# Values of a cross-attention layer made eight heads at a time, with 512 moving columns

## The chip, the cores and the metric

The kernel runs on one core of one Trainium2 chip. The metric is the device time of one execution in microseconds (us); the times of several runs are given with their median.

## What is computed

A cross-attention block and a feed-forward block with low-rank experts, both with a residual, over 16 sequences of 64 tokens and width 512 (1024 tokens in all). Cut to what matters here:

```python
def _L0_xattn_ref(hidden_q, hidden_kv, attention_mask, position_bias, Wq, Wk, Wv, Wo):
    B, S, D, H, DH = (2, 128, 512, 32, 128)
    q = (hidden_q @ Wq).reshape(b, lq, h, dh)
    k = (hidden_kv @ Wk).reshape(b, lk, h, dh)
    v = (hidden_kv @ Wv).reshape(b, lk, h, dh)
    score = jnp.einsum('bqhd,bkhd->bhqk', q, k) * scale + position_bias
    ...
    ctx = jnp.einsum('bhqk,bkhd->bqhd', probs, v).reshape(b, lq, h * dh)
    return ctx @ Wo
x = x + _L0_xattn_ref(_layernorm(x, axis=-1), ctx_4096, ...)
x = x + _L0_ffn_ref(_layernorm(x, axis=-1), ...)
```

`Wk` and `Wv` are 512 x 4096 (32 heads of 128), so keys and values are each a product of 1024 x 512 by 512 x 4096. The change concerns the values.

## The kernel before

**Arithmetic.** Every large product is made with float32r operands that are split into a high and a low part (`split`, L67: ACT copies the high part, DVE subtracts to get the low one), and three matmuls, high x high, low x high and high x low (`mm3`, L219). On top of that, the products of weights and tokens are made by a Winograd-Strassen scheme (`winograd`, L176): each matrix is cut into 2 x 2 blocks, seven block products are made instead of eight (`ORDER`: 1, 2, 6, 5, 7, 4, 3), and sums of blocks are taken before (classes `Tokens`, L115, and `Weights`, L149) and after (`post`, L180). A pass works on n output blocks side by side. Block k has an x bank in PSUM for products 1, 6, 7 and 4, a z bank for product 2 and a y bank for products 5 and 3. After product 1, ACT copies x to `u`; after 2, DVE adds u and z to the block c11; after 6, ACT copies x to `u2`; after 7, ACT copies x to `u3` and DVE adds u3 and y to c22; after 4, ACT copies x out as c21; after 3, DVE adds u2 and y to c12. The next product into a bank waits for the copy before it.

**Stages.** `cT` holds the context, transposed. Its token parts `t1` to `t7` (high and low) are made once. Then the heads are taken by quads, eight of them.

- Keys of a quad (`mm_weights`, L225, two blocks): the weights stand in the array, 512 tokens move; 7 x 2 x 2 x 3 = 84 matmuls of 512 columns. Blocks are stored to the DRAM tiles `kd` (L303).
- Values of a quad (`mm_tokens`, L232, two blocks, each of two column ranges `r`): 128 tokens stand in the array, 256 weight columns move; 7 x 2 x 2 x 2 x 3 = 168 matmuls of 256 columns. Blocks are stored to the DRAM tiles `vd` (L309), one of which holds two heads.

Quad 0's keys and values are made product by product in turn (L321), while the token parts are still being made. For quads 1 to 7 (L332) keys come first, then values; values of quad 7 come after this loop, interleaved with the first queries (L494). During the values of quads 2 to 5, the eight tiles of x are loaded and normalized (`x_tile`, L284) and transposed on PE (`x_turn`, L294): one after product 6 and one after product 7. `xT` is read later, on POOL, to make the token parts of x for the queries.

After that come attention and output projection in a loop over 16 pairs of heads (L504), where keys, values, queries' weights and biases are loaded again, and then the feed-forward block (from L544).

**What sets the order.** The order on PE in this part is that of the program text (`manual_schedule` for PE). On ACT, DVE, POOL and SP a scheduler sets a fixed order when the kernel is built. All loads and stores here are issued on SP. Buffers come from pools: `raw` (10) for loaded weights, `sum` (4) for sums of weight blocks, `g` (18) for split weights, `o` (9) for token differences at this stage, `sn` (8) for u copies, `ob` (8) for finished blocks, `v` (5) for tiles of x and later values. PSUM has eight banks: six of the pool `psp` (`bank`) and two of the pool `pss` (`small_bank`, used by x's transposes and by z and y of quad 0's values).

Of the kernel before, what the change touches and what calls it, by code (L numbers as in the profile page):

```python
# [9 lines left out]
F32 = mybir.dt.float32  # L10
F32R = mybir.dt.float32r
# [7 lines left out]
P = 128  # L19
# [23 lines left out]


@with_exitstack
def xattn_ffn_kernel(ctx: ExitStack, tc: tile.TileContext, x, ctxT, wq, wk, wv, wo, fside, mask,
                     base_wT, base_b, arT, router_b, lora_b, expert_map, out):
    nc = tc.nc
    scale = 1.0 / math.sqrt(128.0)
# [8 lines left out]
        pools[n] = ctx.enter_context(tc.tile_pool(name=n, bufs=BLOCKS[n]))  # L58
    psp = ctx.enter_context(tc.tile_pool(name="psp", bufs=6, space=PSUM))

    def bank():
        return psp.tile([P, 512], F32, tag="ps", name="ps")

    def blk(tag, name, dt=F32, shape=(P, 512)):
        return pools[tag].tile(list(shape), dt, tag=tag, name=name)

    def split(hi, lo, src, lo_eng=None):  # L67
        nc.scalar.copy(hi, src)  # L68
        (lo_eng or nc.vector).tensor_tensor(lo, src, hi.bitcast(F32), ALU.subtract)  # L69
# [30 lines left out]
            nc.tensor.transpose(ps[:, kc * P:(kc + 1) * P], xn[:, kc * P:(kc + 1) * P], ident)  # L100

    kd = [dram.tile([P, TOK], F32, tag=f"kd{h}", name=f"kd{h}") for h in range(H)]
    vd = [dram.tile([P, NT, 256], F32, tag=f"vd{h}", name=f"vd{h}") for h in range(H // 2)]

    with ExitStack() as actx:
        pss = actx.enter_context(tc.tile_pool(name="pss", bufs=2, space=PSUM))
# [5 lines left out]
        def small_bank(name):  # L112
            return pss.tile([P, 512], F32, tag="s", name=name)

        class Tokens(dict):  # L115


            def __init__(self, src, eng):
                self.eng, self.t = eng, {}
                lo, hi = slice(0, HALF), slice(HALF, TOK)  # L120
                self.b = {(i, j): [src[:, 2 * i + k, c] for k in range(2)] for i in range(2)
                          for j, c in enumerate((lo, hi))}
# [26 lines left out]
        class Weights(dict):  # L149
# [5 lines left out]
            def summed(self, a, b, op, name):  # L155
                r = blk("sum", name, F32, (P, 2, self.cols))
                self.eng.tensor_tensor(r, a, b, op)  # L157
                return r
# [12 lines left out]
            def all(self, order=ORDER):  # L171
                for i in order:
                    self.make(i)
                return self

        def winograd(mm, n, emit, yzbank=bank, order=ORDER):  # L176

            xb, zb, yb, u, u2, u3 = ({} for _ in range(6))

            def post(i, k):  # L180
                if i == 1:
                    u[k] = blk("sn", "u")
                    nc.scalar.copy(u[k], xb[k])
                elif i == 2:
                    c = blk("ob", "c11")
                    nc.vector.tensor_tensor(c, u[k], zb[k], ALU.add)
                    emit(0, 0, k, c)
                elif i == 6:
                    u2[k] = blk("sn", "u2")
                    nc.scalar.copy(u2[k], xb[k])  # L190
                elif i == 7:
                    u3[k] = blk("sn", "u3")
                    nc.scalar.copy(u3[k], xb[k])
                    c = blk("ob", "c22")
                    nc.vector.tensor_tensor(c, u3[k], yb[k], ALU.add)
                    emit(1, 1, k, c)
                elif i == 4:
                    c = blk("ob", "c21")
                    nc.scalar.copy(c, xb[k])
                    emit(1, 0, k, c)  # L200
                elif i == 3:
                    c = blk("ob", "c12")
                    nc.vector.tensor_tensor(c, u2[k], yb[k], ALU.add)
                    emit(0, 1, k, c)

            for i in order:
                for k in range(n):
                    if i == 1:
                        xb[k] = bank()
                    elif i == 2:  # L210
                        zb[k] = yzbank()
                    elif i == 5:
                        yb[k] = yzbank()
                    b = xb if i in (1, 6, 7, 4) else zb if i == 2 else yb
                    mm(i, k, b[k], i in (1, 2, 5))
                    post(i, k)
                yield i
# [7 lines left out]
        def mm_weights(t, g):  # L225
            def mm(i, k, o, first):
                for kc in range(2):
                    mm3(o, [a[:, kc, k * P:(k + 1) * P] for a in g[i]], [b[:, kc] for b in t[i]],
                        first and kc == 0, kc == 1)
            return mm  # L230

        def mm_tokens(t, g):  # L232
            def mm(i, k, o, first):
                for r in range(2):
                    c = slice((2 * k + r) * P, (2 * k + r + 1) * P)
                    for kc in range(2):
                        mm3(o[:, r * 256:(r + 1) * 256], [a[:, kc, c] for a in t[i]],
                            [b[:, kc] for b in g[i]], first and kc == 0 and r == 0, kc == 1)
            return mm

        def load_raw(src):
            r = {}
            for i, j in ((0, 0), (0, 1), (1, 0), (1, 1)):
                r[i, j] = blk("raw", "raw", F32, (P, 2, 256))
                nc.sync.dma_start(out=r[i, j], in_=src[i, j])
            return r

        def gran4(r, eng):
            return Weights(r[0, 0], r[0, 1], r[1, 0], r[1, 1], 256, eng)
# [34 lines left out]
        def x_tile(t):  # L284
            nonlocal xT
            if xT is None:
                xT = ax.tile([P, KC, TOK], F32, tag="ax", name="xT")
            xt = blk("v", "xt")
            nc.sync.dma_start(out=xt, in_=x[t])
            xn = blk("v", "xn")  # L290
            norm(sm, [xn], [xt])
            return xn

        def x_turn(t, xn):  # L294
            ps = small_bank("pst")
            transposed(ps, xn)
            b, g = divmod(t, 4)
            dst = xT.rearrange("p k (g a b s) -> p g b k a s", g=4, a=2, b=2)[:, g, b]
            nc.scalar.copy(dst, ps.rearrange("p (k a s) -> p k a s", k=KC, a=2))

        def emit_k(q):
            def emit(i, j, k, c):
                nc.sync.dma_start(out=kd[4 * q + 2 * i + k][:, j * HALF:(j + 1) * HALF], in_=c)  # L303
            return emit

        def emit_v(q):
            def emit(i, j, k, c):
                t = 4 * j + 2 * k
                nc.sync.dma_start(out=vd[2 * q + i][:, t:t + 2, :], in_=c.rearrange("p (t d) -> p t d", t=2))  # L309
            return emit  # L310

        tc_ = Tokens(cT, nc.vector)
# [1 line left out]
        with tc.manual_schedule(engines={nc.tensor.engine}):  # L314
# [2 lines left out]
                tc_.make(i)  # L317
                gv.make(i)
            keys = winograd(mm_weights(tc_, gk), 2, emit_k(0))
            values = winograd(mm_tokens(tc_, gv), 2, emit_v(0), lambda: small_bank("yzv"))  # L320
            for n in range(7):  # L321
                if n < 6:
                    gk.make(ORDER[n + 1])
                    tc_.make(ORDER[n + 1])
                    gv.make(ORDER[n + 1])
                else:
                    rk = load_raw(wk[1])
                    rv = load_raw(wv[1])
                    gk = gran4(rk, nc.vector).all()
                next(keys)  # L330
                next(values)
            for q in range(1, NQ):  # L332
                gv = gran4(rv, nc.vector).all()
                if q + 1 < NQ:
                    rk = load_raw(wk[q + 1])
                    rv = load_raw(wv[q + 1])
                for i in winograd(mm_weights(tc_, gk), 2, emit_k(q)):
                    pass
                if q + 1 < NQ:
                    gk = gran4(rk, nc.vector).all()  # L340
                if q == 2:
                    nc.vector.tensor_scalar(maskb, m8, -1.0, BIG, ALU.add, ALU.mult)  # L342
                    nc.vector.tensor_reduce(valid, m8, AX.X, ALU.max)
                    nc.vector.tensor_copy(emf, emi)
                    for e in range(E):
                        nc.vector.tensor_scalar(oneh[:, e, :], emf, float(e), 2.0, ALU.is_equal, ALU.mult)
                if q + 1 < NQ:
                    for i in winograd(mm_tokens(tc_, gv), 2, emit_v(q)):
                        if 2 <= q < 6:
                            t = 2 * (q - 2)  # L350
                            if i in (1, 5):
                                xn = x_tile(t + (i == 5))
                            elif i in (6, 7):
                                x_turn(t + (i == 7), xn)


            acc = None
# [17 lines left out]
            def load_v(p):  # L375
                v = []
                for w in range(4):
                    v.append(blk("v", "v", F32, (P, 2, 256)))
                    nc.sync.dma_start(out=v[w], in_=vd[p][:, 2 * w:2 * w + 2, :])
                return v  # L380

            def load_o(p):
# [326 lines left out]
```

## Time and profile before

| | |
|---|---|
| runs (3) | 793.59, 793.68, 794.07 us; median 793.68 |
| profiled execution, its own time | 795.94 us |
| its span | 794.2 us |
| PE busy in the span | 778.5 us |
| DVE, ACT, POOL busy | 589.1, 413.0, 144.0 us |
| keys of quad 2 on PE | 89.08 to 108.14 us |
| values of quad 1 on PE | 68.92 to 89.08 us |
| first attention scores on the chain that ended last | 338.07 us |

The profile is of one execution. Matmuls overlap, so their durations add up to more than the time they take; the distance from one start to the next is what a matmul costs in a dense stretch. A row of the timeline reads: start, duration, engine, line, operation, output<-inputs, shape, count, and in brackets the idle time before it with what ended that.

### The profile page before, as it was taken

What the parts mean: (1) busy time and instruction counts of PE and PEld (TensorE: products, weight loads), DVE (VectorE), ACT (ScalarE), POOL (GpSimd) and SP (SyncE); (2) the same over time, 40 slices, a digit from 0 to 9 for tenths busy, and PEclk for the clock granted to TensorE, in tenths of its full rate; (3) what the DMA queues carried; (4) which work ended last, traced back from release to release, by engine and by line L of the source; (5) the groups of instructions that cost most, each with busy time, mean ns of one, the idle gap of its engine ahead of it and who ended that gap; (6) DMA issues with size and microseconds to landing.
All of it is one profiled execution on the core that took longest, in us unless ns stands there. A gap on an engine that the chain in (4) does not pass through costs nothing.

```text
span 794.2 us, 18002 instructions
## 1 busy us (share of the span) xinstructions
PE 778.5 (98%) x6944; PEld 673.7 (85%) x6944; DVE 589.1 (74%) x1056; ACT 413.0 (52%) x1154; POOL 144.0 (18%) x146
## 2 busy tenths in 40 slices
PE   7999999999999999999999999999999999999997
PEld 6988999999999999978888888888888888888786
DVE  6997656555557555678878787878777887878986
ACT  6655444454444444674664566455655466456342
POOL 1011000000006002033311332033202230210352
PEclk9999999999999999999999999999999999999999
DMA  7675545454545543375553364335553455241011
GB/s 269 207 244 200 173 159 186 160 186 160 185 160 171 174 159 133 127 237 170 173 170 90 129 186 161 107 124 171 161 157 97 147 175 171 84 148 56 1 42 66
DMA packets 66374, 120.56 MB, mean 152 GB/s; under 512 B 7536, under 2 KB 8176, under 8 KB 66288
## 3 DMA queue, kind: packets, MB, share of 16 engines
q1 hardware_dynamic: 66288, 119.42, 45.8%
q8 instruction: 54, 0.88, 0.5%
q14 instruction: 32, 0.26, 0.1%
HBM read 83.74 MB, written 35.65 MB: 150 GB/s over the span
## 4 chain that ended last, share of the span: by engine, by line
PE 88%; DVE 7%; ACT 2%; DMA 2%; issue 1%; POOL 0%; SPq 0%; ACTq 0%; DVEq 0%; POOLq 0%
PE ps L222 77%; PE pss L404 4%; PE ps L436 4%; PE pst L423 2%; PE yzv L222 1%; ACT p L412 1%; DMA cT<-in_ctxT 1%; DVE o L637 1%; DVE pr L606 1%; DVE x2l L69 1%; DVE nb L94 1%; DVE gl L69 0%; PE pst L100 0%; DVE we L608 0%; DMA so<-in_wo 0%
## 5 line engine op out<-in xcount | busy, mean ns | idle before, releaser
L68 ACT CAST gh<-s 128x512 fp32r<-128x512 f32 (+1 forms) x128 | 65.6, 514 | 147.3 <-PE ps L222 139.3
L69 DVE TENSOR_TENSOR gl<-s,gh 128x512 fp32r<-128x512 f32 (+1 forms) x128 | 73.3, 572 | 44.5 <-ACT gh L68 44.4
L452 DVE TENSOR_TENSOR acc<-acc,ps 128x512 f32<-128x512 f32 x128 | 86.1, 681 | 21.6 <-PE ps L222 20.7
L412 ACT ACTIVATE p<-p,nm 128x64 f32<-128x64 f32 x256 | 85.5, 336 | 31.6 <-DVE nm L409 31.6
L222 PE MATMUL ps<-wh,oh 128*128 128x512 f32 x256 | 101.4, 397 | 0.0
L222 PE MATMUL ps<-wl,oh 128*128 128x512 f32 x256 | 99.9, 391 | 0.0
L222 PE MATMUL ps<-wh,ol 128*128 128x512 f32 x256 | 99.7, 390 | 0.0
L157 POOL TENSOR_TENSOR s<-rq 128x256 f32<-128x256 f32 x32 | 25.2, 788 | 290.4 <-DMA rq<-in_wq 206.5
L395 POOL TENSOR_TENSOR bm<-bm,maskb 128x512 f32<-128x512 f32 x32 | 50.0, 1582 | 73.1 <-DVE maskb L342 40.8
L69 DVE TENSOR_TENSOR gl<-raw,gh 128x512 fp32r<-128x512 f32 x48 | 34.1, 712 | 31.4 <-ACT gh L68 31.4
L222 PEld LDWEIGHTS ps<-wl,oh 128*128 128x128 f32 x256 | 48.1, 188 | 10.1
L222 PEld LDWEIGHTS ps<-wh,ol 128*128 128x128 f32 x256 | 48.1, 188 | 9.9 <-DVE ol L69 0.5
L222 PEld LDWEIGHTS ps<-wh,oh 128*128 128x128 f32 x256 | 48.1, 188 | 9.5
L68 ACT CAST gh<-raw 128x512 fp32r<-128x512 f32 x48 | 29.7, 621 | 47.8 <-PE ps L222 36.6
L69 DVE TENSOR_TENSOR ol<-ps,oh 128x512 fp32r<-128x512 f32 x64 | 39.8, 683 | 15.6 <-ACT oh L68 15.6
L412 ACT ACTIVATION_READ_ACCUMULATOR p<-p,nm 128x1 f32 x256 | 48.1, 188 | 0.0
L69 DVE TENSOR_TENSOR gl<-rq,gh 128x256 fp32r<-128x256 f32 x48 | 32.9, 687 | 11.4 <-ACT gh L68 11.4
L479 DVE TENSOR_TENSOR q<-u,ps 128x512 f32<-128x512 f32 x48 | 32.6, 680 | 10.6 <-PE ps L222 10.6
L68 ACT CAST oh<-ps 128x512 fp32r<-128x512 f32 x64 | 33.1, 590 | 7.7 <-PE ps L436 7.7
L92 POOL TENSOR_TENSOR rs<-rs,nhalf 128x1 f32<-128x1 f32 x16 | 9.5, 595 | 152.1 <-DVE rs L91 109.2
L404 PEld LDWEIGHTS pss<-kT,q 128*64 128x64 f32 x1024 | 31.2, 138 | 5.6 <-PE ps L222 5.0
L436 PEld LDWEIGHTS ps<-pt,v 64*64 64x64 f32 x2048 | 31.4, 135 | 3.3 <-ACT gh L68 2.2
(226 smaller groups left out, 2273.7 us busy)
## 6 DMA issues: line engine op xcount, KB each, us to landing
kd<-c SPq DMA_DIRECT2D x64, 256.0 KB, 2.6
vd<-c SPq DMA_DIRECT2D x64, 256.0 KB, 2.8
v<-vd SPq DMA_DIRECT2D x64, 256.0 KB, 4.3
kT<-kd SPq DMA_DIRECT2D x64, 256.0 KB, 5.4
raw<-in_wk SPq DMA_DIRECT2D x32, 256.0 KB, 3.0
raw<-in_wv SPq DMA_DIRECT2D x32, 256.0 KB, 3.0
bm<-in_fside SPq DMA_DIRECT2D x32, 256.0 KB, 5.7
rq<-in_wq SPq DMA_DIRECT2D x32, 256.0 KB, 5.5
```

The lines of the kernel that those rows point to most:

```text
L68: nc.scalar.copy(hi, src)
L69: (lo_eng or nc.vector).tensor_tensor(lo, src, hi.bitcast(F32), ALU.subtract)
L92: nc.gpsimd.tensor_tensor(rs, rs, nhalf[:, 0:n], ALU.pow)
L157: self.eng.tensor_tensor(r, a, b, op)
L222: nc.tensor.matmul(o, lhsT=a, rhs=b, start=first and n == 0, stop=last and n == 2, skip_group_check=True)
L395: nc.gpsimd.tensor_tensor(bm, bm, maskb, ALU.add)
L404: nc.tensor.matmul(ps[a * S:(a + 1) * S, t, :], lhsT=qT[n // 8][:, c], rhs=kT[n // 8][:, c], start=True, stop=True)
L412: nc.scalar.activation(p[:, t, :], p[:, t, :], AF.Exp, bias=nm[:, t:t + 1], accum_out=sme[:, t:t + 1])
L423: nc.tensor.transpose(ps[:, g * P:(g + 1) * P], p[:, 2 * g:2 * g + 2, :].rearrange("p t k -> p (t k)"), ident)
L436: nc.tensor.matmul(ps[b][d:d + S, u * S:(u + 1) * S], lhsT=v[u // 2][r, u % 2, c], rhs=pt[r, u, :], start=True, stop=True)
L452: nc.vector.tensor_tensor(acc[:, t, :], acc[:, t, :], ps, ALU.add)
L479: nc.vector.tensor_tensor(self.blocks[key], s[u], b[bk], ALU.add)
```

## The change

The values of quads 1 to 6 are made for two quads together, in three passes. A new class `OctWeights` loads the weights of eight heads (`wvo`, eight loads of 256 KB per pass) into buffers of the pool `o`, sums their blocks and splits them; each of its matrices is two tiles of 128 x 512, one for each half of the depth. The new `mm_oct` has 128 tokens standing and 512 weight columns moving. A pass has four blocks; z and y of blocks 0 and 1 lie in `psp`, those of blocks 2 and 3 in `pss`. The fourth sum of weight blocks is written over the second. Keys of two quads come first, then the values of both. `vd` becomes one tile per quad, and a block is stored to it in rows of 1 KB. Values of quad 0 and of quad 7 stay as they are. Loading, normalization and transposes of x move to the keys of quads 3 to 6: tiles are asked for after products 1 and 6 and transposed after products 5 and 3.

```diff
-    vd = [dram.tile([P, NT, 256], F32, tag=f"vd{h}", name=f"vd{h}") for h in range(H // 2)]
+    vd = [dram.tile([P, 2, NT, 256], F32, tag=f"vd{q}", name=f"vd{q}") for q in range(NQ)]
...
+        class OctWeights(dict):
+            def __init__(self, src):
+                self.a = {}
+                for i, j in ((0, 0), (0, 1), (1, 0), (1, 1)):
+                    self.a[i, j] = [blk("o", "raw8") for _ in range(2)]
+                    for kc in range(2):
+                        nc.sync.dma_start(out=self.a[i, j][kc], in_=src[i, j, :, kc])
+            def summed(self, a, b, op, r=None):
+                r = r or [blk("sum", "s8") for _ in range(2)]
+                for kc in range(2):
+                    nc.vector.tensor_tensor(r[kc], a[kc], b[kc], op)
+                return r
+            def make(self, i):
+                a = self.a
+                if i == 6:
+                    self.s1 = self.summed(a[1, 0], a[1, 1], ALU.add)
+                    self.s2 = self.summed(self.s1, a[0, 0], ALU.subtract)
+                src = (a[0, 0] if i == 1 else a[0, 1] if i == 2 else self.s2 if i == 6 else self.s1 if i == 5 else
+                       self.summed(a[0, 0], a[1, 0], ALU.subtract) if i == 7 else a[1, 1] if i == 4 else
+                       self.summed(a[0, 1], self.s2, ALU.subtract, self.s2))
+                self[i] = [[blk("g", f"g{c}", F32R) for _ in range(2)] for c in "hl"]
+                for kc in range(2):
+                    split(self[i][0][kc], self[i][1][kc], src[kc])
...
+        def mm_oct(t, g):
+            def mm(i, k, o, first):
+                for kc in range(2):
+                    mm3(o, [a[:, kc, k * P:(k + 1) * P] for a in t[i]], [b[kc] for b in g[i]],
+                        first and kc == 0, kc == 1)
+            return mm
...
-                nc.sync.dma_start(out=vd[2 * q + i][:, t:t + 2, :], in_=c.rearrange("p (t d) -> p t d", t=2))
+                nc.sync.dma_start(out=vd[q][:, i, t:t + 2, :], in_=c.rearrange("p (t d) -> p t d", t=2))
+            return emit
+        def emit_oct(q):
+            def emit(i, j, k, c):
+                nc.sync.dma_start(out=vd[q + i][:, :, 4 * j + k, :], in_=c.rearrange("p (w d) -> p w d", w=2))
             return emit
...
-            for q in range(1, NQ):
-                gv = gran4(rv, nc.vector).all()
-                if q + 1 < NQ:
-                    rk = load_raw(wk[q + 1])
-                    rv = load_raw(wv[q + 1])
-                for i in winograd(mm_weights(tc_, gk), 2, emit_k(q)):
-                    pass
-                if q + 1 < NQ:
-                    gk = gran4(rk, nc.vector).all()
+            def keys_of(q, g):
+                xn = {}
+                for i in winograd(mm_weights(tc_, g), 2, emit_k(q)):
+                    if 3 <= q < 7:
+                        t = 2 * (q - 3)
+                        if i in (1, 6):
+                            xn[i] = x_tile(t + (i == 6))
+                        elif i == 5:
+                            x_turn(t, xn[1])
+                        elif i == 3:
+                            x_turn(t + 1, xn[6])
+            for q in range(1, NQ - 1, 2):
+                rk = load_raw(wk[q + 1])
+                go = OctWeights(wvo[q // 2])
+                gn = gran4(rk, nc.vector).all()
+                keys_of(q, gk)
+                rk = load_raw(wk[q + 2])
+                go.all()
...
+                keys_of(q + 1, gn)
+                gk = gran4(rk, nc.vector).all()
+                for i in winograd(mm_oct(tc_, go), 4, emit_oct(q), lambda k: bank() if k < 2 else small_bank("yzv")):
+                    pass
+            gv = gran4(load_raw(wv[1]), nc.vector).all()
+            keys_of(NQ - 1, gk)
...
-                if q + 1 < NQ:
-                    for i in winograd(mm_tokens(tc_, gv), 2, emit_v(q)):
-                        if 2 <= q < 6:
-                            t = 2 * (q - 2)
-                            if i in (1, 5):
-                                xn = x_tile(t + (i == 5))
-                            elif i in (6, 7):
-                                x_turn(t + (i == 7), xn)
```

More of the change, by code (lines that the diff above doesn't have):

```diff
@@ L45, in xattn_ffn_kernel @@
 @with_exitstack
-def xattn_ffn_kernel(ctx: ExitStack, tc: tile.TileContext, x, ctxT, wq, wk, wv, wo, fside, mask,
+def xattn_ffn_kernel(ctx: ExitStack, tc: tile.TileContext, x, ctxT, wq, wk, wv, wvo, wo, fside, mask,
                      base_wT, base_b, arT, router_b, lora_b, expert_map, out):
@@ L59, in xattn_ffn_kernel, with bank @@
     psp = ctx.enter_context(tc.tile_pool(name="psp", bufs=6, space=PSUM))
-    def bank():
+    def bank(k=None):
         return psp.tile([P, 512], F32, tag="ps", name="ps")
@@ L174, in all @@
                 return self
+        class OctWeights(dict):
[21 more added lines that the diff above has]
+                    split(self[i][0][kc], self[i][1][kc], src[kc])
+            def all(self):
+                for i in ORDER:
+                    self.make(i)
+                return self
         def winograd(mm, n, emit, yzbank=bank, order=ORDER):
@@ L210, in winograd @@
                     elif i == 2:
-                        zb[k] = yzbank()
+                        zb[k] = yzbank(k)
                     elif i == 5:
-                        yb[k] = yzbank()
+                        yb[k] = yzbank(k)
                     b = xb if i in (1, 6, 7, 4) else zb if i == 2 else yb
@@ L319, in xattn_ffn_kernel @@
             keys = winograd(mm_weights(tc_, gk), 2, emit_k(0))
-            values = winograd(mm_tokens(tc_, gv), 2, emit_v(0), lambda: small_bank("yzv"))
+            values = winograd(mm_tokens(tc_, gv), 2, emit_v(0), lambda k: small_bank("yzv"))
             for n in range(7):
@@ L327, in xattn_ffn_kernel @@
                     rk = load_raw(wk[1])
-                    rv = load_raw(wv[1])
                     gk = gran4(rk, nc.vector).all()
@@ L331, in xattn_ffn_kernel @@
                 next(values)
-            for q in range(1, NQ):
-                gv = gran4(rv, nc.vector).all()
-                if q + 1 < NQ:
-                    rk = load_raw(wk[q + 1])
-                    rv = load_raw(wv[q + 1])
-                for i in winograd(mm_weights(tc_, gk), 2, emit_k(q)):
-                    pass
-                if q + 1 < NQ:
-                    gk = gran4(rk, nc.vector).all()
-                if q == 2:
+            def keys_of(q, g):
[16 more added lines that the diff above has]
+                go.all()
+                if q == 1:
                     nc.vector.tensor_scalar(maskb, m8, -1.0, BIG, ALU.add, ALU.mult)
@@ L378, in load_v @@
                     v.append(blk("v", "v", F32, (P, 2, 256)))
-                    nc.sync.dma_start(out=v[w], in_=vd[p][:, 2 * w:2 * w + 2, :])
+                    nc.sync.dma_start(out=v[w], in_=vd[p // 2][:, p % 2, 2 * w:2 * w + 2, :])
                 return v
@@ L684 @@
         "wk": c(arr(L0_xattn_Wk).reshape(2, 2, P, NQ, 2, 256).transpose(3, 4, 0, 2, 1, 5)),
-        "wv": c(arr(L0_xattn_Wv).reshape(2, 2, P, NQ, 2, 256).transpose(3, 4, 0, 2, 1, 5)),
+        "wv": c(arr(L0_xattn_Wv).reshape(2, 2, P, NQ, 2, 256)[:, :, :, (0, NQ - 1)].transpose(3, 4, 0, 2, 1, 5)),
+        "wvo": c(arr(L0_xattn_Wv)[:, 512:-512].reshape(2, 2, P, NQ // 2 - 1, 2, 512).transpose(3, 4, 0, 2, 1, 5)),
         "wo": c(arr(L0_xattn_Wo).reshape(H // 2, 2, P, D)),
```

## The prediction

> **What bounds the kernel now.** I read the first and fourth part of the page, then a table by stage, then the matmuls one by one where the heads' values are made. The page: TensorE (PE) is busy nearly all the time, and the chain that ended last runs through it.
>
> ```profile
> span 794.2 us, 18002 instructions
> PE 778.5 (98%) x6944; PEld 673.7 (85%) x6944; DVE 589.1 (74%) x1056; ACT 413.0 (52%) x1154; POOL 144.0 (18%) x146
> ...
> PE 88%; DVE 7%; ACT 2%; DMA 2%; issue 1%; POOL 0%; SPq 0%; ACTq 0%; DVEq 0%; POOLq 0%
> ```
>
> The table of busy time by stretch (window: length, then PE, weight load, DVE, ACT, POOL, clock, DMA share, GB/s) shows where PE is not busy, and how much room the others have while values are made (108.14 to 128.30 is one such pass):
>
> ```profile
> 0.00:20.00 20.00, 14.59 (x70) 12.33 (x71) 13.62 (x22) 12.36 (x21) 2.25 (x8) 1.00 0.78 267
> ...
> 60.00:64.00 4.00, 2.88 (x13) 2.08 (x12) 2.50 (x12) 2.01 (x4) 0.55 (x1) 1.00 0.45 137
> 108.14:128.30 20.16, 20.16 (x170) 20.15 (x169) 11.83 (x21) 11.00 (x19) 0.88 (x1) 1.00 0.48 162
> ```
>
> Between 64 and 325 us PE has no gap: there a microsecond less of PE work is a microsecond less of span, as long as nothing else becomes late. What a matmul costs is not its duration (they overlap) but the distance from start to start. The timeline of PE where keys (512 moving columns) give way to values (256):
>
> ```profile
> 107.46 0.39 PE L222 MATMUL ps<-t3h,gh 128*128 128x512 f32 x1
> 107.69 0.39 PE L222 MATMUL ps<-t3h,gl 128*128 128x512 f32 x1
> 107.92 0.39 PE L222 MATMUL ps<-t3l,gh 128*128 128x512 f32 x1
> 108.14 0.28 PE L222 MATMUL ps<-gh,t1h 128*128 128x256 f32 x1
> 108.26 0.28 PE L222 MATMUL ps<-gh,t1l 128*128 128x256 f32 x1
> 108.38 0.28 PE L222 MATMUL ps<-gl,t1h 128*128 128x256 f32 x1
> ```
>
> Over whole passes: values of quad 1 run from 68.92 to 89.08, 20.16 us for 168 matmuls, 0.1200 each; keys of quad 2 from 89.08 to 108.14, 19.06 us for 84, 0.2269 each. Twice 0.1200 is 0.2400: two 256-column matmuls cost 0.0131 us more than one of 512. Each matmul carries some 0.013 us whatever its width.
>
> [...]
>
> **The change part by part.**
>
> *Matmuls.* Six quads' values go: 6 x 168 = 1008 matmuls of 256 columns, 6 x 20.16 = 120.96 us. Three passes for eight heads come, each 7 products x 4 token blocks x 2 halves of the depth x 3 = 168 of 512 columns: 3 x 168 x 0.2269 = 114.36 us. Stationary and moving operands are the same float32r tiles as in the keys' and values' passes, so 0.2269 is taken (bounds: 0.2267, the spacing in steady flow, to 0.2290, that of the 512-column matmuls at 63.7 us when the operands had just been made: 114.26 to 115.42). **Sum: -6.60 us** (-6.70 to -5.54). The compiled order of the changed program confirms it: PE has 504 rows fewer.
>
> *Evictions, splits and sums* (ACT copies of 0.58 and 0.62 us, DVE of 0.68 to 0.71): as many and as wide as before, 953 rows on DVE in both orders, POOL's unchanged. They lie beside PE: in the pass above DVE is busy 11.83 and ACT 11.00 of 20.16 us; per quad this now falls into 19.06 (62% and 58%). Cost 0. If the cover were gone, each late one would stop PE by its lateness.
>
> *PSUM.* The eight-head pass has four x blocks and four z or y blocks open, which is all eight banks: none is spare. I went through the changed program's order with its waits, and counted the matmuls between the last one that an eviction (with all that stands before it on its engine) depends on, and the one that needs it. In the eight-head passes that is 18 or more (18 x 0.2269 = 4.1 us for one or two operations of 0.6 to 0.7). The least anywhere is 6 (1.36 us): the u3 copy between products 7 and 4 of the keys, as before. Cost 0, to 1.1 per border in a rival below.
>
> *The split ring.* g has 18 buffers; a product of the eight-head pass takes 4 instead of 2, so splits run 4.5 products ahead (24.5 us) instead of 9 (25.9). Cost 0.
>
> *Weight loads* of values: 48 DMAs of 256 KB on SP before and after; wvo's rows are 2 KB like wv's. They go to the nine o buffers, which hold the token differences until quad 0 is split. The eighth load of the first pass stands on SP behind the store of kd3's c21 block (about 41 us before), and lands in about 3.0 us (row of in_wv), 7.4 at the worst that any DMA of vd took: 44 to 49. Its first reader stands in DVE's order where the sum at 55.24 stood. Cost 0; the price of lateness is a rival. The last quad's wv load now comes after the third pass, 19 us of keys ahead of its use. The eight token differences on POOL (244.9 to 257 before) now queue for o buffers behind the third pass's weights; they are first read at 311.0, so some 20 us of delay is free.
>
> *Value stores*: 48 of 256 KB, now in 1 KB rather than 2 KB runs. [...] upper bound, twice: 5.6. Four are issued per product of 5.45 us and there are eight ob buffers, so even 5.6 holds nobody. Cost 0.
>
> *Transposes of x.* Four transposes for each of 8 tiles, as before, now within keys, directly before product 7. Their cost on PE:
>
> ```profile
> 116.66 0.28 PE L222 MATMUL ps<-gl,t6h 128*128 128x256 f32 x1
> 116.78 0.60 PE L100 MATMUL pst<-ident,xn 128*128 128x128 f32 x4
> 117.13 0.36 PE L222 MATMUL ps<-gh,t5h 128*128 128x256 f32 x1
> ```
>
> 0.35 us and a slow first matmul, in both places: difference 0. On ACT, though, the copy to xT (0.59) and, for two of the tiles, a next tile's normalization (0.82) now stand before u3. Counting from the start T of the transposes: the transposes end at T+0.60, so xT may start at T+0.65 (the 0.05 is the usual step from PE's end to ACT), the normalization at T+1.13, u3 at T+1.96 (also when product 7's first block is ready), done T+2.5; PE wants it at T+0.43+12x0.227 = T+3.15. Spare 0.6 us. Its statistics come from a DMA issued a tile earlier, 8 to 11 us before. Cost 0, to about 1 us for each of four tiles.
>
> *Left as it is*: the start, the attention stage, the tail, and the one stall in this stage:
>
> ```profile
> 61.80 0.16 DVE L94 SCALAR_TENSOR_TENSOR nb<-mv,rs 128x1 f32<-128x1 f32 x1 [0.73 <-POOL rs L92]
> 61.99 0.81 ACT L96 ACTIVATE xn<-xt,nb,rs 128x512 f32<-128x512 f32 x1 [2.08 <-DVE nb L94]
> 62.71 0.56 ACT L193 COPY u<-ps 128x512 f32<-128x512 f32 x1
> ...
> 63.33 0.50 PE L222 MATMUL ps<-t4h,gh 128*128 128x512 f32 x1 [1.12 <-ACT u L193]
> ```
>
> The u3 copy waits behind x tile 0's normalization, that behind DVE, which had worked without a gap since about 20 us. The changed order has the same sequence there, with s8 sums in place of s sums: the 1.12 us stay.
>
> **Sum.** Profiled execution 795.94 us (span 794.2 and 1.7 around it): 795.94 - 6.60 = 789.34, span 787.6. It lies 2.26 above the median of the runs, 793.68; on the median: **787.1**. A measurement of this kernel can tell about 0.2%, 1.6 us, from no change.
>
> **The rivals.**
>
> *Better: the stall goes too.* If the other load order relieves DVE before 62 us, 1.12 us more: 786.0. Against: same order of work on DVE. 7%.
>
> *Bank borders.* PE waits at the entry and exit of each eight-head pass, six times up to 1.12 (the one late eviction that the trace has): 793.8 in full, 790.4 at half. For: no bank is free. Against: the count of 18 matmuls. 12%, of which 4% within 0.2%.
>
> *Transposes hold u3.* Up to 1 us for four tiles: 788.1 to 791.1, say 789. For: 0.6 us to spare. Against: only two of the four carry a normalization. 6%.
>
> *Slower: the first pass's weights block DVE.* [...] If the eighth load lands after 55.2, DVE stands with key splits and c blocks behind it, and PE stops 1:1. It decides from 55.2 + 6.6 = 61.8 (even) and shows as slower from 63.4, 22 us after its issue; at 66 us it gives 787.1 + 10.8 = 797.9. For: 2 MB are now wanted early, beside the keys' weights, with DMA engines at 0.86 share at 40 to 44 us. Against: 6 to 11 us of margin. 7%.
>
> That the change doesn't do what it says is excluded by the 504 rows.
>
> **Numbers.** Forecast 68%, own range 786.4 to 788.2 (the matmul bounds). Range for 8 in 10: 785.8 to 790.5, leaving out the upper half of the borders' case and the slower one. Faster .68+.07+.08+.06 = 0.89; same 0.04; slower 0.07.
>
> **What would show it.** PE rows of 128x512 with t stationary spaced 0.227 us, 38.1 us a pass; no PE wait over 0.3 us between 64 and 318 us; attention's first scores about 6.6 us earlier than 338.07. Wrong, if PE waits on ACT u3 after transposes, on c blocks at a pass's border, or DVE on raw8 near 55 us; or if spacing with t stationary isn't that of the keys.

## The result, and the profile after

| | before | after |
|---|---|---|
| runs (6 each) | 792.71 to 794.07, median 793.59 us | 786.57 to 790.51, median 788.46 us |
| ratio of the times, 95% interval | | 0.9938 [0.9921, 0.9955] |
| profiled execution, its own time (span) | 795.94 (794.2) us | 787.93 (786.1) us |

The change makes the kernel 5.1 us faster by the medians, where 6.6 were forecast. Two more comparisons of the same kernels gave 0.9932 [0.9914, 0.995] and 0.9928 [0.9912, 0.9943]. The forecast amounts to a ratio of 787.1/793.68 = 0.9917: just outside the first interval, inside the other two.

Span, busy times of the engines and shares of the chain that ended last, from the page of after:

```profile
span 786.1 us, 16982 instructions
PE 770.8 (98%) x6440; PEld 646.0 (82%) x6440; DVE 586.2 (75%) x1056; ACT 414.0 (53%) x1154; POOL 143.2 (18%) x146
...
PE 86%; DVE 7%; ACT 3%; DMA 1%; issue 1%; POOL 0%; SPq 0%; DVEq 0%; ACTq 0%; POOLq 0%
```

PE has 504 instructions fewer and is 7.7 us less busy. DVE has the same number of instructions, ACT and POOL too. Now the table by stretch of after, with the columns of the forecast's table; the last three rows are the three eight-head passes:

```profile
60.00:64.00 4.00, 3.38 (x15) 2.48 (x14) 3.26 (x6) 2.80 (x5) 0.00 (x0) 1.00 0.36 131
85.87:123.95 38.08, 38.08 (x170) 31.54 (x168) 21.64 (x34) 17.26 (x30) 0.00 (x0) 1.00 0.57 177
163.83:202.01 38.18, 38.18 (x171) 31.63 (x170) 21.44 (x33) 18.17 (x32) 0.00 (x0) 1.00 0.53 175
241.90:280.08 38.18, 38.18 (x171) 31.63 (x170) 25.66 (x33) 17.47 (x31) 11.89 (x8) 1.00 0.46 150
```

The first two numbers of each pass are equal: PE is busy from end to end. Together they last 114.44 us (114.36 forecast). DVE, the busiest of the others, is busy 57 to 67% of a pass. The matmuls one by one, where keys give way to the first eight-head pass (timeline of after, PE):

```profile
85.42 0.39 PE L255 MATMUL ps<-t3h,gl 128*128 128x512 f32 x1
85.64 0.39 PE L255 MATMUL ps<-t3l,gh 128*128 128x512 f32 x1
85.87 0.39 PE L255 MATMUL ps<-gh,t1h 128*128 128x512 f32 x1
86.09 0.39 PE L255 MATMUL ps<-gh,t1l 128*128 128x512 f32 x1
```

The start-to-start distance stays 0.22 to 0.23 us across the border, whichever operand stands in the array. The waits of PE in after between 9 and 320 us (what waited, on what: us in all, times, longest):

```profile
PE ps L255 <- ACT u L226: 0.6, 1, 0.6
PE ps L255 <- DVE gl L69: 0.2, 1, 0.2
```

Neither lies at a border of a pass; between 64 and 320 us there is none. The first is the stall that the forecast left in place. It is shorter in this execution, 0.62 us where the profile before had 1.12, but its rows (timeline of after) read as before: PE waits for the u3 copy, which stands on ACT behind an x tile's normalization:

```profile
59.92 0.82 ACT L96 ACTIVATE xn<-xt,nb,rs 128x512 f32<-128x512 f32 x1 [1.57 <-DVE nb L94]
60.64 0.56 ACT L226 COPY u<-ps 128x512 f32<-128x512 f32 x1
...
61.26 0.50 PE L255 MATMUL ps<-t4h,gh 128*128 128x512 f32 x1 [0.62 <-ACT u L226]
```

**Where the time came from.** Two marks cut the profiled execution in three: the first matmul of quad 1's keys, and the first scores of attention. Both are starts on PE's timeline.

| kernel | keys of quad 1 begin | first scores | span | between the marks | after the scores |
|---|---|---|---|---|---|
| before | 48.42 | 338.00 | 794.2 | 289.58 | 456.2 |
| after | 46.84 | 329.52 | 786.1 | 282.68 | 456.6 |
| after, two other executions | 48.87, 46.31 | 331.99, 328.72 | 788.6, 784.0 | 283.12, 282.41 | 456.6, 455.2 |

Between the marks 6.90 us went. The stall lies between them, and it took 1.12 us in the profile before and 0.62 in this one: without it the difference is 6.40 us. The passes alone give 6.65. In the first experiment that undoes the width the same three passes last 121.09 us (the forecast's count was 6 x 20.16 = 120.96), and 121.09 - 114.44 = 6.65. The 0.25 us between 6.65 and 6.40 is about what the moved transposes cost (see that experiment).

The rest of the 8.1 us between these two spans can't be put down to the change. The start differs by 1.6 us between them, but the changed kernel's own starts differ by 2.6, and in the experiment that moves only the transposes, where the start is the old one, quad 1's keys begin at 46.81.

### The profile page after: what moved, and what is told of

Read it like the earlier page. It is cut to its first block, busy times and chain, and to the rows that moved or that the text cites. A ratio compares the mean times of both kernels' runs of the same rounds, so it can differ in the third digit from the quotient of the medians.

```text
span 786.1 us, 16982 instructions
## 1 busy us (share of the span) xinstructions
PE 770.8 (98%) x6440; PEld 646.0 (82%) x6440; DVE 586.2 (75%) x1056; ACT 414.0 (53%) x1154; POOL 143.2 (18%) x146
## 4 chain that ended last, share of the span: by engine, by line
PE 86%; DVE 7%; ACT 3%; DMA 1%; issue 1%; POOL 0%; SPq 0%; DVEq 0%; ACTq 0%; POOLq 0%
PE ps L255 71%; PE ps L488 4%; PE yzv L255 4%; PE pss L456 4%; PE pst L475 2%; ACT p L464 1%; DVE gl L69 1%; DMA raw<-in_wv 1%; DVE nb L94 1%; DVE o L689 1%; DVE x2l L69 0%; DVE s L157 0%; PE pst L100 0%; DMA raw<-in_wvo 0%; PE ps L636 0%
## 5 line engine op out<-in xcount | busy, mean ns | idle before, releaser
L469 DVE TENSOR_TENSOR p<-p,rc 128x512 f32<-128x512 f32 x32 | 34.5, 1078 | 1.1
L69 DVE TENSOR_TENSOR gl<-rq,gh 128x256 fp32r<-128x256 f32 x48 | 26.4, 551 | 11.4 <-ACT gh L68 11.4
```

What stands on the lines that cost most here:

```text
L469: nc.vector.tensor_tensor(p, p, rc.unsqueeze(2).to_broadcast([P, NT, S]), ALU.mult)
```

## The experiments

The theory after the result: the whole gain is the width of the matmuls in three passes; everything else in the change costs nothing, and what differs besides is the spread from execution to execution. The rivals: part of the gain comes from the order of loads and stores, or from the place of x's transposes; part of the forecast 6.6 us is given back somewhere.

### The changed kernel again

Edit: none. Six executions, then a single one, then six on another chip.

> The changed kernel once more, for a tighter interval and a second trace. Theory A (what was forecast: 504 fewer matmuls, each saving its fixed 0.013 us, all of it on the path): 6.6 us below the kernel before, 787.0 to 787.5, ratio 0.9917. Theory B (part of it is given back by waits that differ from one execution to the next, so that the median gain stays near the 5.1 us of the first six runs): 788 to 789, and the trace shows, beside passes of 38.1 us, waits of PE in the first 64 us or after 300 us that the first trace of it does not have.

> The changed kernel, one more execution for its trace. Theory A: span near 785.5, stage boundaries as in the first trace. Theory B: a different span with the difference in one place, the first 64 us (DVE without a gap there, waiting for weights or slowed while POOL works) or the entry of attention.

> The changed kernel beside the run with all values in eight-head passes, on one chip. Theory A: 787 to 789, ratio 0.992 to 0.994; the spread between executions again comes from the first 64 us and the entry of attention.

Measured: 788.8 us against 794.46 (0.9932 [0.9914, 0.995]); 785.73 for the single one; 788.86 against 794.33 (0.9928 [0.9912, 0.9943]). The first number is the one that theory B named, not theory A's 787.0 to 787.5. All 19 executions of the changed kernel lie between 785.73 and 790.51, those of the kernel before, over all comparisons, between 791.95 and 797.7: single executions of one kernel differ by 4.8 and 5.8 us, about as much as the gain. Two of the profiles show where. First the longer one's rows on PE (the first re-run, 788.6 us of span), at the start and at the old stall:

```profile
7.38 0.80 PE L255 MATMUL ps<-t1h,gh 128*128 128x512 f32 x1 [1.04 <-ACT t1h L68]
...
63.79 0.50 PE L255 MATMUL ps<-t4h,gh 128*128 128x512 f32 x1 [1.13 <-ACT u L226]
```

Then the same two matmuls in the shorter one (784.0 us of span):

```profile
6.26 0.80 PE L255 MATMUL ps<-t1h,gh 128*128 128x512 f32 x1
...
60.47 0.51 PE L255 MATMUL ps<-t4h,gh 128*128 128x512 f32 x1 [0.37 <-ACT u L226]
```

In one PE waits 1.04 us for the split of a part of the context, for which ACT had itself waited 2.07 us until it landed (0.93 in the other, where PE doesn't wait); the stall at 60 to 64 us is 1.13 us in one and 0.37 in the other. A third place comes after the first scores: 10 to 13 us behind them PE waits for a u copy and then, in most profiles, for a sum on DVE, 1.80 us together in the longer execution and 0.56 in the shorter. (The single execution's 784.0 us of span, against 786.1 in the first profile, comes mostly from here: 455.2 and 456.6 us after the first scores.) These are waits of the kind that theory B asked for. But the kernel before has them too (0.66, 1.12 and 1.41 us in its profile), so they don't show that the change gives something back.

The start comes in two kinds. In ten profiles, of both kernels and of the experiments, it has quad 0's values in it. In four of them (the kernel before, the first re-run and two experiments) two operations on DVE last 1.8 us beside POOL near 45 us, and quad 1's keys begin at 47.7 to 48.9 us; in the six others two last 1.2 us, and the keys begin at 46.3 to 47.7. The stall at 60 to 64 us was 1.1 us wherever it followed the first kind, 0.2 to 0.7 after the second. DVE has hardly a gap there, so 2 x 0.6 us more on it may well be the reason; no run sets it on purpose. The last section shows the rows.

PE's work in the start and after the first scores is the same in both kernels. (Of the loads beside it, the change takes those of quad 1's value weights out of the start, and reads the values from the new tiles.) After the first scores the executions of both take between 455.2 and 456.6 us. So a difference of two single spans (8.1 us above) says less than the stretch between the marks, which is 282.2 to 283.1 us in four executions, and 282.0 to 282.1 in all four once the stall is taken off.

### The width undone

```diff
-                for kc in range(2):
-                    mm3(o, [a[:, kc, k * P:(k + 1) * P] for a in t[i]], [b[kc] for b in g[i]],
-                        first and kc == 0, kc == 1)
+                for r in range(2):
+                    w = slice(r * 256, (r + 1) * 256)
+                    for kc in range(2):
+                        mm3(o[:, w], [a[:, kc, k * P:(k + 1) * P] for a in t[i]], [b[kc][:, w] for b in g[i]],
+                            first and kc == 0 and r == 0, kc == 1)
```

Eight heads, loads, stores, sums and transposes stay as changed; each matmul of 512 columns becomes two of 256.

> The changed kernel, but with each 512-column matmul of the eight-head passes split into two of 256: passes, buffers, banks, loads, stores and transposes stay as changed, only the 504 matmuls come back. Theory A: 6.6 us slower than the changed kernel, so level with the kernel before (ratio 0.998 to 1.002), 20.16 us more precisely 40.3 us a pass. Theory C (the gain comes from the new order of the work and of the loads in the first 64 us, not from the matmuls): nearly as fast as the changed kernel, ratio 0.994.

Measured: 794.36 us against 794.46, ratio 1.0001 [0.9993, 1.0009]. The first pass in the table by stretch of this kernel:

```profile
85.83:126.14 40.31, 40.31 (x337) 40.31 (x336) 21.43 (x33) 16.66 (x30) 0.00 (x0) 1.00 0.51 168
```

It lasts 40.31 us for 336 matmuls, 0.1200 each, as in the kernel before; the stretch between the marks is 289.37 (289.58 before). The gain is gone, all of it. That settles the main question: the width is the gain, and the other parts of the change together cost or bring less than 0.1% (the interval). The third number differs too: weight loading is busy the whole of this pass (40.31 us), and 31.5 of 38.1 us of the wide one. Half the loads go with half the matmuls, so this run doesn't tell whether the time saved is the matmuls' own or that of their weight loads.

### The transposes alone

The kernel before, with load, normalization and transposes of x moved from the values to the keys.

```diff
                 for i in winograd(mm_weights(tc_, gk), 2, emit_k(q)):
-                    pass
+                    if 3 <= q < 7:
+                        t = 2 * (q - 3)
+                        if i in (1, 6):
+                            xn[i] = x_tile(t + (i == 6))
+                        elif i == 5:
+                            x_turn(t, xn[1])
+                        elif i == 3:
+                            x_turn(t + 1, xn[6])
...
                     for i in winograd(mm_tokens(tc_, gv), 2, emit_v(q)):
-                        if 2 <= q < 6:
...
+                        pass
```

> The kernel before with one part of the change alone: loading, normalization and transposes of x moved from the values to the keys, in the places that the change gives them. Theory A: no difference, ratio 0.999 to 1.001, no wait of PE on ACT u copies after the transposes. Rival (the copy to xT and the next normalization hold the u3 copy): up to 1 us for each of four tiles, 794.5 to 797.5, with idle PE before product 4 of the keys of quads 3 to 6.

Measured: 793.95 us, ratio 1.0 [0.999, 1.0009]; no wait of PE between 64 and 320 us. In the times the move is worth nothing either way, and the feared wait doesn't come. The stretch between the marks shows a small price: 289.41 us with a stall of 0.68 in it, so 288.73 without, against 289.58 - 1.12 = 288.46 before. Nearly all of the 0.27 us lies in four passes of values behind keys with transposes, which take 20.22 to 20.23 us where the first takes 20.16; why, no run shows. Why nothing becomes late is seen in after, where the transposes begin at 134.83 (timeline of after, rows of PE, then of ACT):

```profile
134.60 0.39 PE L255 MATMUL ps<-t5l,gh 128*128 128x512 f32 x1
134.83 0.60 PE L100 MATMUL pst<-ident,xn 128*128 128x128 f32 x4
135.19 0.48 PE L255 MATMUL ps<-t7h,gh 128*128 128x512 f32 x1
...
138.04 0.39 PE L255 MATMUL ps<-t4h,gh 128*128 128x512 f32 x1
...
135.47 0.59 ACT L339 COPY xT<-pst 128x512 f32<-128x512 f32 x1
135.95 0.81 ACT L96 ACTIVATE xn<-xt,nb,rs 128x512 f32<-128x512 f32 x1
136.86 0.59 ACT L226 COPY u<-ps 128x512 f32<-128x512 f32 x1
```

From T = 134.83: xT at T+0.64, the next tile's normalization at T+1.12, u3 from T+2.03 to T+2.62, and PE needs it at T+3.21. The forecast had 0.65, 1.13, 1.96 to 2.5, and 3.15: 0.6 us to spare, in both.

### Other widths

The forecast said that each matmul carries some 0.013 us whatever its width. That is an estimate from its two distances: between 0.1200 us for 256 columns and 0.2269 for 512 lies 0.1069/256, some 1/2400 us a column, and over that 0.013 us are left at both. Two kernels test the sentence, with one execution each. The first cuts each matmul of 512 columns into four of 128 (the loop of the width's edit, with `r` in `range(4)` and `P` columns), the second into 384 and 128:

```diff
...
+                for n, w in enumerate((slice(0, 384), slice(384, 512))):
+                    for kc in range(2):
+                        mm3(o[:, w], [a[:, kc, k * P:(k + 1) * P] for a in t[i]], [b[kc][:, w] for b in g[i]],
+                            first and kc == 0 and n == 0, kc == 1)
```

> The changed kernel with each 512-column matmul of the eight-head passes split into four of 128 columns (2016 matmuls in place of 504). It tells what the 0.013 us are. Theory A (each matmul carries about 0.0133 us beside 1/2400 us per column, so 128 columns take 0.0667): a pass of 44.8 us instead of 38.1, 20 us slower in all, near 806. Rival (256 columns already stand at a floor that the load of the 128 stationary columns sets, 0.120 us whatever the width): a pass of 80.6 us, 127 us slower, near 915.

> The changed kernel with each 512-column matmul of the eight-head passes split into one of 384 and one of 128 columns: a third width. The run with four times 128 gave 0.1117 us per 128-column matmul, so the simple form (0.0133 us and 1/2400 us per column at every width) is already wrong at 128. Theory A in its narrower form [...]: 0.1733 for 384 columns and a pass of 168 x (0.1733 + 0.1117) = 47.9 us. Rival (the load always adds part of its time, the more the narrower the matmul): spacing for 384 columns above 0.178.

Measured: 899.74 and 819.06 us. The first lies at neither of the two numbers named, 806 and 915, though much nearer the second. The first pass of the kernel with four quarters, from its table by stretch:

```profile
87.25:162.30 75.05, 75.05 (x674) 75.05 (x673) 21.61 (x33) 16.65 (x30) 0.00 (x0) 1.00 0.30 97
```

672 matmuls in 75.05 us are 0.1117 us each; by the sentence they should have taken 128/2400 + 0.013 = 0.067 us. A matmul of 128 columns costs nearly what one of 256 costs (0.1200). Weight loading is busy all of the pass here, its starts 0.11 us apart like the matmuls', so its pace may be what sets that floor. But it is busy all of the pass of 256 columns too (40.31 us), and the record of one load lasts 0.19 us at 128, 256 and 512 columns alike: what holds the narrow matmuls back was not shown. The kernel with 384 and 128 has this first pass and these rows of 384 columns (table by stretch; the timeline of PE follows):

```profile
85.77:134.25 48.48, 48.48 (x338) 48.48 (x336) 21.43 (x33) 16.63 (x30) 0.00 (x0) 1.00 0.44 144
```

```profile
100.34 0.34 PE L255 MATMUL ps<-gh,t6l 128*128 128x384 f32 x1
100.52 0.34 PE L255 MATMUL ps<-gl,t6h 128*128 128x384 f32 x1
100.70 0.22 PE L255 MATMUL ps<-gh,t6h 128*128 128x128 f32 x1
```

Within a run of six, matmuls of 384 columns are 0.18 us apart, where 384/2400 + 0.0133 would be 0.1733; where the width changes, one distance is 0.23 and one 0.06. The pass of 48.48 us is over the 47.9 of the narrower theory, and its rival (more than 0.178) is met only just. The four distances in a row of equal widths are 0.112, 0.120, 0.18 and 0.227 us for 128, 256, 384 and 512 columns. No constant beside N/2400 gives them all: over it lie 0.058, 0.013, 0.020 and 0.014. What law does is left open. For this change only 256 and 512 count, and both were measured in the kernel before.

### The stall at 61 us

In the changed kernel the normalization of x's first tile waits for DVE, which has hardly a gap from 20 to 62 us. Here `nhalf`, a constant that the normalizations need, is made from a block of quad 1's keys, so that they come later; the numbers computed are the same.

```diff
-        nc.gpsimd.memset(nhalf, -0.5)
...
+                if (i, j, k) == (0, 1, 1):
+                    nc.gpsimd.tensor_scalar(nhalf, c[:, 0:NT], 0.0, -0.5, ALU.mult, ALU.add)
```

> The changed kernel, with the exponent of the normalizations of x made from a block of quad 1's keys, so that no normalization can stand ahead of those keys' u3 copies on ACT (numbers that are computed stay the same). Theory A (the wait at 61 us comes from that normalization alone): the 0.4 to 1.1 us wait before product 4 of quad 1's keys is gone, 0.4 to 1.1 us faster than the changed kernel, ratio to the kernel before 0.991 to 0.9925. Rival (DVE's backlog is what is late): u3 waits no longer but c blocks or splits do, and PE still stops for as long in the next two products.

Measured: 788.43 us, ratio 0.9923 [0.9902, 0.9943], no different from the changed kernel's. The wait at 61 us is gone, and this one has come in the keys of quad 2 (timeline, ACT and PE):

```profile
80.31 0.82 ACT L96 ACTIVATE xn<-xt,nb,rs 128x512 f32<-128x512 f32 x1 [1.37 <-DVE nb L94]
81.03 0.56 ACT L226 COPY u<-ps 128x512 f32<-128x512 f32 x1
...
81.65 0.50 PE L255 MATMUL ps<-t4h,gh 128*128 128x512 f32 x1 [0.43 <-ACT u L226]
```

It is the same meeting on ACT, 20 us later: a normalization comes just ahead of a u3 copy whose slack is less than its 0.82 us. DVE has no backlog this time: it had stood idle for 1.39 us before it ran on at 76.96. So the place in ACT's fixed order can make the stall without one. The 0.4 to 1.1 us that were expected did not come: the experiment takes away no time that could be measured.

### All 32 heads wide

If the width is the gain, the two quads left narrow (0 and 7) should give the same again: a fourth eight-head pass for quads 0 and 1, keys of quads 0 and 1 in turn at the start, keys of quad 7 beside the queries.

```diff
-            values = winograd(mm_tokens(tc_, gv), 2, emit_v(0), lambda k: small_bank("yzv"))
+            more = winograd(mm_weights(tc_, gn), 2, emit_k(1), lambda k: small_bank("yzv"))
...
-            for q in range(1, NQ - 1, 2):
...
+            for q in range(0, NQ, 2):
...
-            for n, i in enumerate(winograd(mm_tokens(tc_, gv), 2, emit_v(NQ - 1), order=ORDER_Q)):
+            for n, i in enumerate(winograd(mm_weights(tc_, gk), 2, emit_k(NQ - 1), order=ORDER_Q)):
```

> The same carried on: values of all 32 heads in four eight-head passes. Quad 1's keys take the place of quad 0's values in the interleaved start, quad 7's keys that of quad 7's values beside the queries. 336 matmuls of 256 columns become 168 of 512. Theory A: 2 x 20.16 - 38.14 = 2.2 us less than the changed kernel, 786 to 786.5, ratio to the kernel before about 0.990. Rival (an eight-head pass straight after the start needs weights and splits while DVE has no slack): waits of PE between 46 and 64 us on splits of the first pass that eat the 2.2 us or more, 788 to 793.

The same with the later normalizations of the edit above:

> Both edits: all values in eight-head passes, and normalizations of x not before quad 2's keys are done. Theory A: another 0.4 to 1.1 us below the run with all values in eight-head passes, 785.0 to 786, unless that run has no wait of this kind. Rival: no difference from it.

And once more beside the changed kernel on one chip:

> All values in eight-head passes once more, on the chip of the changed kernel. Theory A: 2.2 us of matmuls and up to 1.1 us of a wait that it doesn't have, 2 to 4.5 us below the changed kernel, ratio to the kernel before 0.987 to 0.990. Rival: the first run of it was a lucky one, and it is level with the changed kernel.

Measured: 784.15 us (0.9868 [0.9847, 0.9889]); with the late normalizations (here from quad 2's keys) 784.67 (0.9881 [0.9859, 0.9903]), no better; again, 784.18 (0.9872 [0.9857, 0.9887]), beside 788.86 for the changed kernel. It beats both kernels. Its first pass (table by stretch):

```profile
46.52:84.78 38.26, 38.26 (x169) 31.39 (x168) 29.53 (x66) 19.00 (x35) 3.01 (x5) 1.00 0.68 219
```

No wait of PE is left between 9 and 320 us: the normalizations now fall into the first pass, where an eviction has 18 matmuls of time (18 x 0.227 = 4.1 us). With the late normalizations one comes back, 0.42 us at 117.35, in the keys of quad 3.

The gain over the changed kernel is 4.7 us by medians, more than expected: one more pass wide instead of narrow is 40.3 - 38.2 = 2.1 us, the stall 0.2 to 1.1, together 2.3 to 3.2. The profiles, three of this kind and four of the changed kernel, differ by 3.6 us on average: 0.9 up to the start of the stretch (45.6 to 47.5 us against 46.3 to 48.9), 2.3 from there to the first scores (280.0 to 280.7 against 282.2 to 283.1) and 0.4 after them. Half of the 2.1 us is due before the stretch, since quad 1's keys (19.06 us) take the place of quad 0's values (20.16) there. Between 0.4 and 1.3 us of the 3.6, and the 1.1 up to 4.7, were not traced to a cause; this kernel's executions spread less (782.8 to 784.81), so a calmer start may be part of it; that is argued, not shown.

## Why the prediction was right

**Matmuls: right.** Forecast -6.60 us, measured -6.65 in the passes; between the marks -6.90 as they stand and -6.40 without the stall. Undoing the width alone brings the ratio to 1.0001. The stretch was PE's alone (in after busy for 38.08 of 38.08 us of the first pass, with no wait from 64 to 320 us), so PE's microseconds were the span's.

**Evictions, splits, sums: right.** As many operations as before, DVE busy for at most 67% of a pass, no wait of PE.

**Bank borders: the rival fell.** No wait of PE at the six borders in any of the four profiles of the changed kernel (none begins between 64 and 320 us), with all eight buffers of `psp` and `pss` open. The count of 18 matmuls between an eviction and the reuse fits that.

**Transposes: right on the waits.** The steps fell within 0.1 us of the forecast's (the end of u3 0.12 later), and the move alone measured 1.0 [0.999, 1.0009]. The difference of 0 on PE was not quite that: about 0.27 us in the traces.

**The first pass's weights: the rival fell.** The eighth load was issued at 39.5 us (41 forecast) and landed at 45.4 (44 to 49 forecast); the sum that waits for it ran at 53.2 us, and DVE waited for no load between 20 and 64 us. It would have had to land after 53.

**Value stores: right in time to landing, one term missed.** The 48 in rows of 1 KB land in 2.8 us by the median, like the stores before. The forecast's upper bound of 5.6, twice those 2.8 us, held for all of them (4.6 at most). What the forecast did not name is SP: a store in rows of 1 KB keeps it 0.51 us, one in rows of 2 KB 0.32. These are after's rows for the eight-head blocks and for the others (duration of one: least, median, most, in ns, then first and last start):

```profile
L354 SPq DMA_DIRECT2D vd<-c x48: 512/513/1422, 93.9 to 281.4; - x48
...
L349 SPq DMA_DIRECT2D vd<-c x16: 319/323/487, 20.6 to 328.6; - x16
```

48 x 0.19 = 9 us more of SP's time were hidden, as 16 stores (8.2 us of SP) fall into a pass of 38 us. By an estimate from the same figures (4 x 0.19) a load behind four of them goes out 0.8 us later than behind four of the old ones; what that costs where there is less lead was not shown.

**The stall stays: right**, though its size isn't a constant: 0.23 to 1.13 us in four executions of the changed kernel, against the 1.12 that was taken from one of the kernel before.

**What was off.** The median fell by 5.1 to 5.7 us in three comparisons, not 6.6. The stretch between the marks gave nearly what was forecast (6.4 us without the stall), so most of the missing 1 to 1.5 us lies, as far as the traces show, in the spread of the start, the stall and the entry of attention, where the executions of both kernels differ by more than that. The means over all these executions (788.39 us for 19, 794.45 for 63) differ by 6.1 us, more than the medians do; the intervals of the second and third comparison (4.0 to 6.8 us and 4.5 to 7.0) hold 6.6, that of the first (3.6 to 6.3) does not. No run shows the change giving time back outside the stretch, and none excludes half a microsecond. And the sentence on "some 0.013 us whatever its width" was wrong as a law: it was read from two widths and does not hold at 128 or 384. The sum was safe because it used the two distances themselves.

## What to carry to other kernels

Where one engine is busy from end to end, price a change by the start-to-start distance of its instructions in a steady stretch, measured for each shape that the change uses, and don't stretch a rule from two shapes to a third. Compare a stretch between two marks that the change encloses, rather than whole spans, when single executions differ by as much as the change is worth. When an operation is inserted ahead of another in an engine's fixed order, write down the times of the chain from the insertion to the reader: here a spare of 0.6 us, worked out in advance, was what the chip showed.

## What was not expected of the hardware

- A matmul of 128 moving columns costs 0.112 us and one of 256 costs 0.120: with a new weight load for each, hardly anything is gained by going from 256 columns to 128.
- Two operations of DVE lasted 1.2 instead of 0.68 us while POOL added masks to biases. The timelines of POOL and DVE in after show which:

```profile
42.70 4.57 POOL L447 TENSOR_TENSOR bm<-bm,maskb 128x512 f32<-128x512 f32 x2 [39.89 <-DVE maskb L396]
...
43.14 0.68 DVE L157 TENSOR_TENSOR s<-raw 128x512 f32<-128x512 f32 x1
...
44.94 1.19 DVE L69 TENSOR_TENSOR gl<-raw,gh 128x512 fp32r<-128x512 f32 x1
46.05 0.68 DVE L236 TENSOR_TENSOR c<-u,ps 128x512 f32<-128x512 f32 x1
46.65 1.18 DVE L69 TENSOR_TENSOR gl<-s,gh 128x512 fp32r<-128x512 f32 x1
```

The kernel before has two such rows of 1.79 us:

```profile
43.58 3.38 POOL L395 TENSOR_TENSOR bm<-bm,maskb 128x512 f32<-128x512 f32 x2 [40.77 <-DVE maskb L342]
...
44.01 1.79 DVE L157 TENSOR_TENSOR s<-raw 128x512 f32<-128x512 f32 x1
45.72 1.79 DVE L69 TENSOR_TENSOR gl<-s,gh 128x512 fp32r<-128x512 f32 x1
```

Each of the longer rows takes 0.5 us more than 0.68 in after and 1.1 more in the kernel before: in both, the later row ends 0.55 us after POOL's two operations do (47.83 and 47.27, 47.51 and 46.96). But it isn't always DVE that takes longer. The rows at 43.14 and 46.05 lie within POOL's time and kept their 0.68 us; beside the first of them POOL's first operation lasted 2.87 us, against 1.67 in the kernel before. What decides which operation takes longer was not shown.
- SP's time to issue a store of 256 KB was 0.32 us with 128 rows of 2 KB and 0.51 with 256 rows of 1 KB, while the median time to landing was 2.8 us for the stores before and for those of 1 KB. Whether the number of rows or the form of the access makes the difference was not tested.
